# Four graph layers on one core: logit weights by TensorE, three rows of logits spread by TensorE, and layer 0 of two graphs projected ahead of its aggregation

## The chip, the cores and the metric

The kernel runs on one core of a Trainium2 chip. The metric is the device time of one launch in microseconds (us). Five engines work side by side, each through its own queue in order: TensorE (PE, with its weight loads shown as PEld), VectorE (DVE), ScalarE (ACT), GpSimd (POOL) and SyncE (SP), which here issues every DMA.

## The reference

There are 64 graphs of 256 nodes with 512 features each, all in float32. Each of four layers normalises x, takes the positive part h, computes a graph layer from h and the adjacency matrix, and adds the result to x:

```python
h = jnp.maximum(_layernorm(x, axis=-1), 0.0)
x = x + layer(h, adj, ...)
# layer 0: attention
Wh = h @ W
e = leaky_relu(Wh @ a[:512] + swapaxes(Wh @ a[512:], 1, 2), 0.2)
attention = softmax(where(adj > 0.5, e, -9e15), axis=1)
out0 = elu(attention @ Wh)
# layer 1: normalised adjacency
dh = rsqrt(sum(adj + I, -1));  out1 = relu((dh * (adj + I) * dh) @ h @ kernel1 + bias)
# layer 2: plain
out2 = relu((adj @ h) @ kernel2)        # rows of x that are all zero are masked
# layer 3: mean and self
out3 = relu(concat([h, adj @ h / deg]) @ W3.T)
```

## The kernel before, in words

**Tiles.** A graph is 2 chunks of 128 nodes. x of a graph stays in SBUF (`xs`) through all four layers. A layer 0, 1 or 2 is an aggregation (`aggregate`, L450) and a projection (`project`, L511). The aggregation multiplies h as the stationary operand with the moving 256 columns of the attention or the adjacency, so its result `pt` has features on the partitions, in two PSUM banks; ACT and DVE evict it into `xw` (`left_sums`, L436). The projection multiplies `xw` with the weights in seven products of half size instead of eight (a scheme of Strassen's kind). It needs sums of blocks on both sides: S1 to S4 of `xw` (DVE at L445 and L428, POOL at L432), and the differences T1 to T4N of each weight, which POOL makes once at the start (`weight_sums`, L285, the instructions at L290). Three PSUM banks z, v and y collect the products (L529); ACT keeps copies (L568) and DVE adds (L570). Layer 3 projects first and then aggregates.

**Layer 0.** `norm(0)` gives h0. Four DVE operations (L628) multiply h0 with the rows of `wa`, which is W a spread over all partitions, and sum along the features: the two logits `lg` of each node. One of them must lie as a row on all partitions. `along` (L347) does that: a DVE transpose (L355), a DMA to DRAM (L358), and a DMA that reads the row back to all partitions (L361). Then ACT adds the other logit and takes the leaky relu (L634), DVE masks (L642) and takes the maximum (L645), ACT exponentiates (L649), DVE inverts the sum (L652), ACT scales (L655), and `e` is the attention. `aggregate("h0", "e", 0)` and the projection follow, and `elu0` adds the ELU of the result to x in three pieces, of 256, 256 and 512 columns.

**The logit weights.** `logit_weights` (L253) makes `wa` ahead of everything: it loads W0 a second time in four blocks of rows (L259) and both halves of a, each read to all partitions (L263); eight DVE operations (L270) multiply and sum along a row into columns; eight TensorE transposes of a broadcast column (`spread`, L242, recorded at L244) lay them as rows on all partitions in PSUM, and ACT copies them to `wa` (L282).

**The order of the work.** Nothing is issued where it is written. Each step is registered with `op` (L217): its engine, a planned duration, a function, the keys that it reads and writes. `Plan.place` (L70) then simulates the engines: a planned duration is multiplied by STRETCH of its engine, due times are passed backwards from those of each graph (APART us from graph to graph, the last LAST graphs closer together by LATE), and at each point the engine takes the step that can start first, then the one that is due first; for TensorE a step counts as ready only SPARE us after its inputs. Buffers are given out in the same simulation, from the numbers at L819. Steps are then emitted in order of their planned start, so each engine's order is fixed; the chip's own waits do the rest.

```python
rank = (max(free[eng], ready + spare), not op.urgent, op.due, op.at)
```

Of the kernel before, what the change touches and what calls it, by code (L numbers as in the profile page):

```python
# [11 lines left out]
ALU = mybir.AluOpType  # L12
AX = mybir.AxisListType

P = 128
# [6 lines left out]
HOP = 0.25  # L22
APART = 12.0
LAST, LATE = 2, 0.3

STRETCH = {"DVE": 1.25, "ACT": 1.15, "POOL": 1.2, "PE": 1.0, "DMA": 1.0}
SPARE = 0.15

# [121 lines left out]
def kernel(  # L150
# [21 lines left out]
    nc = tc.nc  # L172
    B, N, F = x.shape
    O = w0.shape[1]
    NC = N // P
# [14 lines left out]
    class Tiles:  # L190
# [5 lines left out]
        def declare(self, name, shape, pool=None, tag=None):  # L196
            tag = pool or tag or name
            self.tiles[name] = Buffered(shape, tag, f"{name}_{self.name}")
# [43 lines left out]
    def spread(to, col):  # L242

        nc.tensor.transpose(to, col.to_broadcast([P, P]), ident)  # L244
# [7 lines left out]

    def logit_weights():  # L253
        me = Tiles("l", 0.0)
        op, declare = me.op, me.declare
        declare("wa_col", [P, 2, FC])
        for k in range(FC):
            declare(f"w0{k}", [P, O], tag="xw")
            op("DMA", 256, lambda g, k=k: nc.sync.dma_start(  # L259
                g[f"w0{k}"], w0[k * P : (k + 1) * P, :]), (), [f"w0{k}"])  # L260
        for j in range(2):
            declare(f"a{j}", [P, O], tag="ex512")
            op("DMA", 256, lambda g, j=j: nc.sync.dma_start(  # L263
                g[f"a{j}"],
                a0[j * O : (j + 1) * O, :].rearrange("o u -> u o").to_broadcast([P, O])),
               (), [f"a{j}"])
        for k in range(FC):
            for j in range(2):
                declare(f"junk{j}{k}", [P, O], tag="mva")
                op("DVE", 0.77, lambda g, j=j, k=k: nc.vector.scalar_tensor_tensor(  # L270
                    g[f"junk{j}{k}"], g[f"w0{k}"], 1.0, g[f"a{j}"], ALU.mult, ALU.mult,
                    accum_out=g["wa_col"][:, j, k : k + 1]),
                   [f"w0{k}", f"a{j}"], [f"junk{j}{k}", f"wa_col.{j}"])
        for j in range(2):
            declare(f"pw{j}", [P, F], "ps")

            def go(g, j=j):
                for k in range(FC):
                    spread(g[f"pw{j}"][:, k * P : (k + 1) * P], g["wa_col"][:, j, k : k + 1])

            op("PE", 0.6, go, [f"wa_col.{j}", "=ident"], [f"pw{j}"])
            op("ACT", 0.59, lambda g, j=j: nc.scalar.copy(wa[:, j, :], g[f"pw{j}"]),  # L282
               [f"pw{j}"], [f"=wa{j}"])

    def weight_sums(op, n, b12):  # L285
# [8 lines left out]
    def weight(n, w):  # L294
# [3 lines left out]
        for at, i, j in ((B11, 0, 0), (None, 0, 1), (B22, 1, 1), (B21, 1, 0)):  # L298
# [5 lines left out]
                  (), ["b12" if at is None else f"=wb{n}.{at}"])  # L304
        weight_sums(me.op, n, "b12")

    def last_weight():
# [34 lines left out]
    def graph(b):  # L342
# [283 lines left out]
        for j in range(2):  # L626
            for c in range(NC):
# [3 lines left out]
                   [f"h0.{c}", f"=wa{j}"], ["e.0", "e.1", f"lg.{j}{c}"])  # L631
        along("pl", lambda g: g["lg"][:, 0, :], ["lg.00", "lg.01"])
        for c in range(NC):
# [20 lines left out]
        for c in range(NC):  # L654
            op("ACT", 0.5, lambda g, c=c: nc.scalar.activation(  # L655
                g["e"][:, c, :], g["e"][:, c, :], AF.Copy, scale=g["den"][:, c : c + 1]),
               [f"e.{c}", f"den.{c}"], [f"e.{c}", "e"])
        aggregate("h0", "e", 0)

# [15 lines left out]
        first, second, third = pieces(0)  # L675
        project([Weighted("xw0", 0)], 0, plain_keep, 0.38, plain_total, lambda _: elu0(*first, "a"))
        elu0(*second, "b")
        elu0(*third, "c")
        norm(1, "dh")
# [131 lines left out]
    constants()  # L811
    logit_weights()
    weight(0, w0)
# [3 lines left out]
    for b in range(B):  # L817
        graph(b)
    buffers = dict(  # L819
        xs=7, a_nat=1, ab=1, aT=6, h=3, mva=6, xw=5, c=3, off=1, junk=1, ex256=3, ex512=2,  # L820
        wa_col=1, turned=1, row=4, pl=1, pr=1, hb=1, ps=8,
    )
# [36 lines left out]
```

## Time and profile before

| | |
|---|---|
| median of 3 runs | 2843.36 us (2842.63 to 2843.51) |
| the profiled execution: time, span from first to last instruction | 2844.11 us, 2842.3 us |
| granted TensorE clock | 0.999 |
| DMA over the span | 161.07 MB, 57 GB/s; 189 GB/s from 0 to 5 us, 311 GB/s from 5 to 10 us |
| TensorE busy from 0 to 30 us | 3.75 us |
| TensorE busy from 142 to 2700 us | all but 0.4 us |

The page of a profile gives each engine's busy time and its share of the span. A row of a group or of the timeline names the engine, the line, the operation and its operands, how many there are and how long; in square brackets stands the idle time before it and what ended it. A float32 product of TensorE is recorded as two instructions; a transpose is one. A busy time of TensorE includes the drain of each instruction, so the distance from start to start (0.22 us for 256 columns) is the time that counts, not the 379 ns of a record.

### The profile page before, as it was taken

To read this page: it belongs to the slowest core of one execution; us is meant where nothing else is said; L and a number is where in the kernel's file an instruction comes from. 1 tells how busy PE (TensorE), PEld (TensorE's weight loads), DVE (VectorE), ACT (ScalarE), POOL (GpSimd) and SP (SyncE) were. 2 spreads that over 40 slices of the span, in tenths; PEclk is the share of its full clock that TensorE was granted. 3 is DMA by queue.
4 is the path that set the end of the run, shared out by engine and by line. 5 is a ranking of instruction groups with operands and counts; after the bars stand their busy time and mean duration, and the time that the engine had idled before them with its cause. 6 is when DMAs were issued, how large, how long until landed. Compare 5 with 4: busy or idle time off the path is not lost.

```text
span 2842.3 us, 43136 instructions
## 1 busy us (share of the span) xinstructions
PE 2802.9 (99%) x12968; PEld 2461.2 (87%) x12968; DVE 1963.5 (69%) x5136; ACT 1691.1 (59%) x4115; POOL 1246.4 (44%) x2331
## 2 busy tenths in 40 slices
PE   5999999999999999999999999999999999999999
PEld 4888888888888888888888888888888888888887
DVE  7767676676766767667676667676776766667654
ACT  5766566556666566566565665665665656556552
POOL 6554344444444444444444444444444444443432
PEclk9999999999999999999999999999999999999999
DMA  7122331222222222222222222222222222222112
GB/s 199 20 51 61 72 70 40 62 53 53 58 53 58 56 49 59 61 45 61 46 62 56 47 66 55 48 59 56 53 59 47 60 53 40 58 49 44 39 34 52
DMA packets 495062, 161.07 MB, mean 57 GB/s; under 512 B 424816, under 2 KB 460656, under 8 KB 494832
## 3 DMA queue, kind: packets, MB, share of 16 engines
q1 hardware_dynamic: 494832, 158.33, 24.0%
q8 instruction: 105, 1.72, 0.3%
q14 instruction: 125, 1.02, 0.1%
HBM read 90.96 MB, written 33.69 MB: 44 GB/s over the span
## 4 chain that ended last, share of the span: by engine, by line
PE 97%; DMA 1%; DVE 1%; POOL 0%; SPq 0%; issue 0%; ACT 0%; DVEq 0%; POOLq 0%
PE pz L529 43%; PE pt L460 23%; PE pv L529 21%; PE py L529 11%; POOL wb L290 0%; DMA xs<-in_x_dram 0%; DMA ab<-in_adj_dram 0%; DVE e L628 0%; SPq L603 0%; DMA wb<-in_L_gnn_W_dram 0%; DVE e L642 0%; DMA pr<-dpr 0%; DVE xw L445 0%; SPq L259 0%; DVE stats L385 0%
## 5 line engine op out<-in xcount | busy, mean ns | idle before, releaser
L529 PE MATMUL pz<-wb,xw 128*128 128x256 f32 x3072 | 767.9, 379 | 2.5 <-DVE c L694 0.6
L529 PEld LDWEIGHTS pz<-wb,xw 128*128 128x128 f32 x3072 | 582.9, 190 | 83.9 <-ACT c L568 1.1
L568 ACT COPY c<-pz 128x256 f32<-128x256 f32 x576 | 213.6, 371 | 550.9 <-PE pz L529 550.3
L529 PE MATMUL pz<-wb,hw 128*128 128x256 f32 x2048 | 524.8, 379 | 0.9 <-ACT c L568 0.9
L432 POOL TENSOR_TENSOR xw<-xw 128x256 f32<-128x256 f32 x384 | 296.1, 791 | 482.1 <-DVE xw L428 326.5
L529 PEld LDWEIGHTS pz<-wb,hw 128*128 128x128 f32 x2048 | 389.0, 190 | 54.5 <-ACT c L568 1.7
L422 ACT ACTIVATE h<-xs,nb,rstd 128x512 f32<-128x512 f32 x512 | 402.1, 809 | 45.5 <-POOL nb L419 39.7
L529 PE MATMUL pv<-wb,xw 128*128 128x256 f32 x1536 | 393.7, 379 | 1.7 <-DVE xw L445 1.1
L529 PEld LDWEIGHTS pv<-wb,xw 128*128 128x128 f32 x1536 | 291.5, 190 | 41.9 <-POOL wb L290 1.5
L570 DVE TENSOR_TENSOR c<-pv,c 128x256 f32<-128x256 f32 x384 | 161.7, 421 | 222.3 <-PE pv L529 150.4
L401 ACT ACTIVATE h<-xs,mv 128x512 f32<-128x512 f32 x384 | 275.4, 718 | 56.1 <-POOL mv L395 36.3
L529 PE MATMUL pv<-wb,hw 128*128 128x256 f32 x1024 | 262.8, 379 | 0.0
L460 PE MATMUL pt<-e,h 128*128 128x256 f32 x1024 | 233.8, 381 | 15.8 <-ACT e L655 15.8
L460 PE MATMUL pt<-aT,h 128*128 128x256 f32 x1024 | 236.9, 379 | 0.0
L460 PE MATMUL pt<-ahT,h 128*128 128x256 f32 x1024 | 233.1, 379 | 0.0
L460 PEld LDWEIGHTS pt<-e,h 128*128 128x128 f32 x1024 | 195.8, 191 | 43.0 <-ACT e L655 16.1
L409 POOL TENSOR_TENSOR rstd<-rstd,minus_half 128x2 f32<-128x2 f32 x256 | 215.9, 843 | 17.3
L460 PEld LDWEIGHTS pt<-aT,h 128*128 128x128 f32 x1024 | 194.5, 190 | 26.7 <-ACT h L422 0.3
L460 PEld LDWEIGHTS pt<-ahT,h 128*128 128x128 f32 x1024 | 194.6, 190 | 26.5
L529 PEld LDWEIGHTS pv<-wb,hw 128*128 128x128 f32 x1024 | 194.5, 190 | 26.5
L628 DVE SCALAR_TENSOR_TENSOR e<-h,wa 128x512 f32<-128x512 f32 x256 | 196.7, 768 | 16.5 <-ACT h L422 5.8
L529 PE MATMUL py<-wb,xw 128*128 128x256 f32 x768 | 197.1, 379 | 0.0
(116 smaller groups left out, 4460.8 us busy)
## 6 DMA issues: line engine op xcount, KB each, us to landing
xs<-in_x_dram SPq DMA_DIRECT2D x64, 512.0 KB
hw<-hb SPq DMA_DIRECT2D x1024, 32.0 KB
out_dram<-xs SPq DMA_DIRECT2D x64, 512.0 KB
ab<-in_adj_dram SPq DMA_DIRECT2D x512, 32.0 KB
a_nat<-in_adj_dram SPq DMA_DIRECT2D x64, 256.0 KB
pl<-dpl SPq DMA_DIRECT2D x64, 128.0 KB
pr<-dpr SPq DMA_DIRECT2D x64, 128.0 KB
w3n_w<-in_L_gnn_W_dram SPq DMA_DIRECT2D x4, 512.0 KB
```

The source lines that it names most:

```text
L401: op("ACT", 1.0, lambda g, c=c: nc.scalar.activation(g[h][:, c, :], g["xs"][:, c, :], AF.Square, bias=g[mv][:, 0, c : c + 1], accum_out=g[ ...
L409: op("POOL", 0.72, lambda g: nc.gpsimd.tensor_tensor(g[rs], g[rs], minus_half, ALU.pow), [rs, "=half"], [rs])
L422: op("ACT", 0.81, lambda g, c=c: nc.scalar.activation(g[h][:, c, :], g["xs"][:, c, :], AF.Relu, bias=g[nb][:, c : c + 1], scale=g[rs][:, c ...
L432: op("POOL", 0.85, lambda g, i=i, o=o: nc.gpsimd.tensor_tensor(g[xw][:, o], g[xw][:, i], g[xw][:, S2], ALU.subtract), put(i, S2), put(o), ...
L460: nc.tensor.matmul(g[pt][:, kk, :], lhsT=g[h][:, c, k * P : (k + 1) * P], rhs=g[moving][:, c, :], start=(c == 0), stop=(c == NC - 1),)
L529: nc.tensor.matmul(g[t], lhsT=o.left(g, left, k), rhs=o.right(g, right, k), start=start and n == 0, stop=n == len(parts) - 1, skip_group_c ...
L568: return "ACT", lambda g, to, block: nc.scalar.copy(to, block)
L570: plain_total = (0.43, lambda g, i, to, block: nc.vector.tensor_tensor(to, block, to, ALU.add))
L628: op("DVE", 0.77, lambda g, j=j, c=c: nc.vector.scalar_tensor_tensor(g["e"].rearrange("p c n -> p (c n)"), g["h0"][:, c, :], 1.0, wa[:, j, ...
```

## The change

W a: `logit_weights` is now called from `weight` for W0, after its differences. It loads a once, as 8 rows of 128, turns them to columns by one transpose, transposes the 16 blocks of W0 (from the tiles that the projection uses), ACT evicts these in four copies, and eight products of 512 columns, with a column of a broadcast as the stationary operand, give W a on all partitions; ACT copies the two halves to `wa`. The second load of W0, the broadcast loads of a and the DVE operations are gone.

Rows of logits: for the first three graphs (ON_PE), two TensorE transposes of a broadcast column put the row into PSUM, where `along` was. Other graphs keep `along`.

Layer 0 of the first two graphs (FIRST): h0 is transposed by TensorE (16 transposes) in the place of the aggregation, then evicted and projected by the same `left_sums` and `project`, into `wh` in SBUF; then for each half of the nodes two products with the attention as the stationary operand and 512 columns of `wh` as the moving one give the layer's result in PSUM, and the ELU takes it in two pieces of 512 columns.

Planner: APART 12 to 14, LAST 2 to 4, smaller STRETCH for DVE, ACT and POOL, SPARE 0.15 to 0.3; one buffer of the tag `ex256` less.

```diff
@@ -20,11 +20,13 @@
 ALPHA = 0.2
 NEG_INF = -9000000000000000.0
 HOP = 0.25
-APART = 12.0
-LAST, LATE = 2, 0.3
-STRETCH = {"DVE": 1.25, "ACT": 1.15, "POOL": 1.2, "PE": 1.0, "DMA": 1.0}
-SPARE = 0.15
+APART = 14.0
+ON_PE = 3
+FIRST = 2
+LAST, LATE = 4, 0.3
+STRETCH = {"DVE": 1.15, "ACT": 1.1, "POOL": 1.15, "PE": 1.0, "DMA": 1.0}
+SPARE = 0.3
@@ -250,38 +252,6 @@
         op("DMA", 256, lambda g: nc.sync.dma_start(
             bias, b1.rearrange("(u o) -> u o", u=1).to_broadcast([P, O])), (), ["=bias"])
-    def logit_weights():
-        me = Tiles("l", 0.0)
-        op, declare = me.op, me.declare
-        declare("wa_col", [P, 2, FC])
-        for k in range(FC):
-            declare(f"w0{k}", [P, O], tag="xw")
-            op("DMA", 256, lambda g, k=k: nc.sync.dma_start(
-                g[f"w0{k}"], w0[k * P : (k + 1) * P, :]), (), [f"w0{k}"])
-        for j in range(2):
-            declare(f"a{j}", [P, O], tag="ex512")
-            op("DMA", 256, lambda g, j=j: nc.sync.dma_start(
-                g[f"a{j}"],
-                a0[j * O : (j + 1) * O, :].rearrange("o u -> u o").to_broadcast([P, O])),
-               (), [f"a{j}"])
-        for k in range(FC):
-            for j in range(2):
-                declare(f"junk{j}{k}", [P, O], tag="mva")
-                op("DVE", 0.77, lambda g, j=j, k=k: nc.vector.scalar_tensor_tensor(
-                    g[f"junk{j}{k}"], g[f"w0{k}"], 1.0, g[f"a{j}"], ALU.mult, ALU.mult,
-                    accum_out=g["wa_col"][:, j, k : k + 1]),
-                   [f"w0{k}", f"a{j}"], [f"junk{j}{k}", f"wa_col.{j}"])
-        for j in range(2):
-            declare(f"pw{j}", [P, F], "ps")
-            def go(g, j=j):
-                for k in range(FC):
-                    spread(g[f"pw{j}"][:, k * P : (k + 1) * P], g["wa_col"][:, j, k : k + 1])
-            op("PE", 0.6, go, [f"wa_col.{j}", "=ident"], [f"pw{j}"])
-            op("ACT", 0.59, lambda g, j=j: nc.scalar.copy(wa[:, j, :], g[f"pw{j}"]),
-               [f"pw{j}"], [f"=wa{j}"])
     def weight_sums(op, n, b12):
         w = wb[n]
         key = lambda i: b12 if i is None else f"=wb{n}.{i}"
@@ -303,6 +273,50 @@
                 g["b12"] if at is None else wb[n][:, at], block),
                   (), ["b12" if at is None else f"=wb{n}.{at}"])
         weight_sums(me.op, n, "b12")
+        if n == 0:
+            logit_weights(me)
+    def logit_weights(me):
+        op, declare = me.op, me.declare
+        OC = O // P
+        declare("a_rows", [2 * OC, P])
+        declare("a_cols", [P, 2 * OC])
+        op("DMA", 4, lambda g: nc.sync.dma_start(
+            g["a_rows"], a0.rearrange("(r p) u -> r (p u)", p=P)), (), ["a_rows"])
+        declare("pa", [P, 2 * OC], "ps")
+        op("PE", 0.15, lambda g: nc.tensor.transpose(
+            g["pa"], g["a_rows"], ident[: 2 * OC, : 2 * OC]), ["a_rows", "=ident"], ["pa"])
+        op("ACT", 0.25, lambda g: nc.scalar.copy(g["a_cols"], g["pa"]), ["pa"], ["a_cols"])
+        blocks = {(0, 0): B11, (0, 1): None, (1, 0): B21, (1, 1): B22}
+        for i in range(OC):
+            declare(f"pw{i}", [P, F], "ps")
+            declare(f"wt{i}", [P, F], tag="aT")
+            for k in range(FC):
+                at = blocks[k // FH, i // (OC // 2)]
+                key = "b12" if at is None else f"=wb0.{at}"
+                def go(g, i=i, k=k, at=at):
+                    block = g["b12"] if at is None else wb[0][:, at]
+                    o = i % (OC // 2) * P
+                    nc.tensor.transpose(
+                        g[f"pw{i}"][:, k * P : (k + 1) * P], block[:, k % FH, o : o + P], ident)
+                op("PE", 0.2, go, [key, "=ident"], [f"pw{i}.{k}"])
+            op("ACT", 0.59, lambda g, i=i: nc.scalar.copy(g[f"wt{i}"], g[f"pw{i}"]),
+               [f"pw{i}.{k}" for k in range(FC)], [f"wt{i}"])
+        for j in range(2):
+            declare(f"pwa{j}", [P, F], "ps")
+            for i in range(OC):
+                op("PE", 0.9, lambda g, i=i, j=j: nc.tensor.matmul(
+                    g[f"pwa{j}"],
+                    lhsT=g["a_cols"][:, j * OC + i : j * OC + i + 1].to_broadcast([P, P]),
+                    rhs=g[f"wt{i}"],
+                    start=i == 0,
+                    stop=i == OC - 1,
+                ), ["a_cols", f"wt{i}"] + ([f"pwa{j}"] if i else []), [f"pwa{j}"])
+            op("ACT", 0.59, lambda g, j=j: nc.scalar.copy(wa[:, j, :], g[f"pwa{j}"]),
+               [f"pwa{j}"], [f"=wa{j}"])
     def last_weight():
@@ -629,7 +643,13 @@
                     g["e"].rearrange("p c n -> p (c n)"), g["h0"][:, c, :], 1.0, wa[:, j, :], ALU.mult, ALU.mult,
                     accum_out=g["lg"][:, j, c : c + 1]),
                    [f"h0.{c}", f"=wa{j}"], ["e.0", "e.1", f"lg.{j}{c}"])
-        along("pl", lambda g: g["lg"][:, 0, :], ["lg.00", "lg.01"])
+        if b < ON_PE:
+            declare("pl", [P, N], "ps")
+            op("PE", 0.23, lambda g: [
+                spread(g["pl"][:, c * P : (c + 1) * P], g["lg"][:, 0, c : c + 1]) for c in range(NC)
+            ], ["lg.00", "lg.01", "=ident"], ["pl"])
+        else:
+            along("pl", lambda g: g["lg"][:, 0, :], ["lg.00", "lg.01"])
         for c in range(NC):
             op("ACT", 0.47, lambda g, c=c: nc.scalar.activation(
                 g["e"][:, c, :], g["pl"], AF.Prelu, bias=g["lg"][:, 1, c : c + 1], alpha=ALPHA),
@@ -655,7 +675,6 @@
             op("ACT", 0.5, lambda g, c=c: nc.scalar.activation(
                 g["e"][:, c, :], g["e"][:, c, :], AF.Copy, scale=g["den"][:, c : c + 1]),
                [f"e.{c}", f"den.{c}"], [f"e.{c}", "e"])
-        aggregate("h0", "e", 0)
         def elu0(i, key, y, y_keys, to, to_keys, n, at, tag):
@@ -673,9 +692,51 @@
                 to(g), g[ex], -1.0, to(g), ALU.add, ALU.add, **kw), [ex], to_keys)
         first, second, third = pieces(0)
-        project([Weighted("xw0", 0)], 0, plain_keep, 0.38, plain_total, lambda _: elu0(*first, "a"))
-        elu0(*second, "b")
-        elu0(*third, "c")
+        if b < FIRST:
+            for half in range(2):
+                pt = f"pt0_{half}"
+                declare(pt, [P, FH, N], "ps")
+                def go(g, half=half, pt=pt):
+                    for k in range(FH):
+                        for c in range(NC):
+                            f0 = (half * FH + k) * P
+                            nc.tensor.transpose(
+                                g[pt][:, k, c * P : (c + 1) * P], g["h0"][:, c, f0 : f0 + P], ident)
+                op("PE", 0.5, go, ["h0.0", "h0.1", "=ident"], [pt])
+            together("pt0_0", "pt0_1")
+            left_sums("pt0_0", "pt0_1", "xw0")
+            declare("wh", [P, NC, O], tag="h")
+            places = {(i, j): (lambda g, i=i, j=j: quarter(g["wh"], i, j), f"wh.{i}{j}")
+                      for i, j in PLACE}
+            project([Weighted("xw0", 0)], 0, plain_keep, 0.38, plain_total,
+                    lambda pz: op("ACT", 0.38, lambda g: nc.scalar.copy(quarter(g["wh"], 1, 0), g[pz]),
+                                  [pz], ["wh.10"], urgent=True), places=places)
+            for i, piece in ((1, second), (0, third)):
+                po = f"po{i}"
+                declare(po, [P, O], "ps")
+                def go(g, i=i, po=po):
+                    for c in range(NC):
+                        nc.tensor.matmul(
+                            g[po],
+                            lhsT=g["e"][:, c, i * P : (i + 1) * P],
+                            rhs=g["wh"][:, c, :],
+                            start=c == 0,
+                            stop=c == NC - 1,
+                        )
+                op("PE", 1.73, go, ["e", "wh.00", "wh.01", "wh.10", "wh.11"], [po])
+                elu0(i, piece[1], lambda g, po=po: g[po], [po],
+                     lambda g, i=i: g["xs"][:, i, :], XS[2 * i : 2 * i + 2], O, piece[-1], "ac"[i])
+            op("POOL", 0.15, lambda g: nc.gpsimd.memset(g["total1"][:, 1:2], 0.0), (), ["total1.10"])
+        else:
+            aggregate("h0", "e", 0)
+            project([Weighted("xw0", 0)], 0, plain_keep, 0.38, plain_total, lambda _: elu0(*first, "a"))
+            elu0(*second, "b")
+            elu0(*third, "c")
         norm(1, "dh")
@@ -809,7 +870,6 @@
     constants()
-    logit_weights()
     weight(0, w0)
     weight(1, w1)
     weight(2, w2)
@@ -817,8 +877,8 @@
     for b in range(B):
         graph(b)
     buffers = dict(
-        xs=7, a_nat=1, ab=1, aT=6, h=3, mva=6, xw=5, c=3, off=1, junk=1, ex256=3, ex512=2,
-        wa_col=1, turned=1, row=4, pl=1, pr=1, hb=1, ps=8,
+        xs=7, a_nat=1, ab=1, aT=6, h=3, mva=6, xw=5, c=3, off=1, junk=1, ex256=2, ex512=2,
+        a_rows=1, a_cols=1, turned=1, row=4, pl=1, pr=1, hb=1, ps=8,
     )
     for tag in ("stats", "total", "mv", "rstd", "nb", "deg", "dh", "rdeg", "lg", "top", "den", "mask"):
         buffers[tag] = 6
```

## The prediction

> **What bounds the kernel now.** I read, in this order, the page (busy shares), the busy time by stretch, TensorE's timeline at the start, its waits, and the timeline of all engines between 14 and 34 us.
>
> ```profile
> PE 2802.9 (99%) x12968; PEld 2461.2 (87%) x12968; DVE 1963.5 (69%) x5136; ACT 1691.1 (59%) x4115; POOL 1246.4 (44%) x2331
> ```
> ```profile
> 10.00:20.00 10.00, 3.31 (x7) 1.27 (x7) 9.23 (x32) 2.69 (x4) 4.35 (x4) 1.00 0.82 234
> 20.00:30.00 10.00, 0.00 (x0) 0.00 (x0) 7.65 (x17) 4.43 (x12) 8.40 (x11) 1.00 0.89 237
> 30.00:40.00 10.00, 6.80 (x22) 5.57 (x23) 7.56 (x17) 5.15 (x13) 9.59 (x12) 1.00 0.78 212
> 40.00:50.00 10.00, 7.33 (x31) 5.24 (x31) 9.83 (x19) 5.77 (x20) 8.18 (x12) 1.00 0.83 233
> ...
> 1000.00:2000.00 1000.00, 1000.00 (x4635) 880.32 (x4634) 699.75 (x1833) 601.92 (x1466) 435.84 (x826) 1.00 0.24 55
> ```
> Columns: stretch, length, then busy us of PE, PEld, DVE, ACT, POOL, clock, DMA share, GB/s. From 142 to 2690 us TensorE never waits; only the start and the last few us leave it idle. So the change can gain only at the start, and it can lose anywhere.
>
> ```profile
> 16.89 0.47 PE L244 MATMUL pw_l<-ident,wa_col_l 128*128 128x128 f32 x1 [1.81 <-DVE junk_l L270]
> 33.20 5.62 PE L460 MATMUL pt<-e,h 128*128 128x256 f32 x16 [15.84 <-ACT e L655]
> 38.66 1.03 PE L529 MATMUL pz<-wb,xw 128*128 128x256 f32 x4
> ...
> 48.44 3.62 PE L460 MATMUL pt<-e,h 128*128 128x256 f32 x16
> 51.89 1.03 PE L529 MATMUL pz<-wb,xw 128*128 128x256 f32 x4
> ```
> ```profile
> PE pt L460 <- ACT e L655: 15.8, 1, 15.8
> PE pw_l L244 <- DVE junk_l L270: 13.2, 5, 9.5
> ```
> The first useful product starts at 33.20, when the attention of graph 0 is done; before it TensorE runs only eight transposes for W a.
>
> ```profile
> 16.01 0.25 DVE L355 STREAM_TRANSPOSE tpl<-lg 128x64 f32<-128x64 f32 x1
> ...
> 16.53 0.67 SPq L358 DMA_DIRECT2D dpl<-tpl  x1
> ...
> 21.88 0.34 SPq L361 DMA_DIRECT2D pl<-dpl  x1
> ...
> 26.22 0.91 ACT L634 ACTIVATE e<-pl,lg 128x256 f32<-128x256 f32 x2 [0.34 <-DMA pl<-dpl]
> ...
> 27.37 0.65 DVE L642 SCALAR_TENSOR_TENSOR e<-off,e 128x512 f32<-128x512 f32 x1
> ...
> 32.66 0.89 ACT L655 ACTIVATE e<-e,den 128x256 f32<-128x256 f32 x2
> ```
> Here the reader sees why: the logits cross to all partitions through DRAM, 16.01 to 26.22, and then max, exponent and division take another 7 us.
>
> **A ledger of TensorE.** 3245 instructions in 700 us (2000 to 2700) give 0.2157 us per pass of 256 columns (a product has two passes). 12,928 such passes make 2789.2, and 32 transposes of the last weight at 0.109 (eight in 0.87) make 3.5: 2792.7 of work. The last product ends at about 2837.4, which leaves 4.9. So 2842.3 = 33.2 before the first product + 2792.7 + 4.9 + 11.5 of gaps. Of the 11.5, 2.0 is a slow first burst (16 passes take 38.66 - 33.20 = 5.46; those at 48.44 take 3.45); the rest lies nearly all before 91.
>
> **What the Trainium skill says.** (1) "TensorE: Matmul & The Clock Gate", Part 1: an idle TensorE runs at half clock until about 3.4 us of activity. The slow burst agrees. (2) Its Part 4 says that transposes don't count as activity. The lone pw_l transposes have a mean of 470 ns, the later pw_w ones 273; that fits, but doesn't separate clock from spacing. (3) "DMA: Bandwidth & Descriptors", Anatomy of one DMA: some 2 us fixed, mostly the write receipt. The trip through DRAM has two such in series and took 10.2 us with its queueing. (4) "GPSIMD Engine Reference", section 8: POOL shares SBUF interfaces with VectorE. L642 took 0.65 us at 27.37, but 1.65 at 39.63 beside a weight difference of POOL.
>
> **The change, part by part.**
>
> *W a on TensorE.* It removes eight L270 operations from VectorE: 8 x (0.678 + 0.083) = 6.1 us, in 8.69 to 16.8, where VectorE is the busy engine. It removes six loads of 256 KB, 1.5 MB, from queues that carry some 235 GB/s then: 6 us of transfer. It adds a load of 4 KB, 16 transposes (1.7 at 0.109; up to 7.5 at the lone 0.47), and 8 products of 512 columns, 16 passes of 2 x 0.2157: 6.9 us warm. ACT gets four more evictions of 0.59 and one small one, 2.6, where it is half idle. Replacing the eight old transposes saves nothing on the path. Is W a ready earlier? x of graph 0 and W0 are 1.5 MB; 189 GB/s to 5 us and 311 after it land that at about 6.8, if they are issued first. Transposes and evictions to 9.5, four products partly cold to 14, copy to 14.6; the second half at 18. The old copies end at 13.1 and 18.0. So not earlier: what it frees is VectorE and the loads.
>
> *Rows by TensorE, graphs 0 to 2.* Removes per graph a 0.24 turn, two DMAs, and the trip of 10.2. Adds two transposes, 0.22, so 0.65 in all, and takes a PSUM bank until the two Prelu have read it. The spread waits on VectorE's two sums; everything planned behind it on TensorE waits too, between 0 and 1.5 us (two L628) per graph. I take 0.5. The second sum of graph 0 (19.5, after wa1) then ends last, not the row: Prelu at 19.5 instead of 26.2; with the 7.0 from there to the product, e comes at about 25.5 to 26.5.
>
> *Layer 0 of graphs 0 and 1 by nodes.* The 16 aggregation passes of 256 (3.45) become 8 of 512 (3.45). The 14 products stay, 6.04. New are 16 transposes each, 1.74, so 3.5. What moves is the projection: it needs h, the weights and POOL's four differences (about 1.5 each after W0 lands: 13 us), not e. So 12.1 us of work can run before e. VectorE's ELU pieces drop from three to two: per graph four passes of 0.69 against two sets of 0.42 + 0.42 + 0.69, 0.4 us with the reads. Each graph holds one more of three h buffers; graph 2's h then waits for graph 0's sums, which end at 19.7, before it is late. ex256 loses a buffer: in steady state ACT waits there for VectorE already, off the path; I cost it at nothing, and up to 0.2 us a graph if that cover is gone.
>
> *Planner constants.* All 64 graphs are reordered, every queue with them, SP's and POOL's too. The stretch on VectorE falls from 1.25 to 1.15, and 0.3 us of slack ahead of a TensorE step stands where 0.15 stood. The steady hw sums (L769 686 ns, L428 639) are planned at 0.43: over the new plan by 0.19 and 0.14, together about the new 0.3. VectorE has 30% free, so I take no cost; bounds from -1 (the end) to +0.3 us per graph, 19 us.
>
> **The sum.** New TensorE work is 1.7 + 6.9 + 0.65 + 3.5 = 12.8. New ledger: start 6.8 + cold 3 (bounds 2 to 6) + 12.8 + 2792.7 + 4.9 = 2820.2 plus gaps. Equal time would need 22.1 of gaps. Before e, 18.7 us stand against 19.5 of work (W a 8.6 + 3 cold, graph 0's transposes and projection 7.8), some of it waiting for POOL and evictions: 4 of gap. After e, I take the 9.5 of before: the same chains feed the same layers. Total 2833.7, so 8.6 less. A cross-check from VectorE, over 90% busy in the tens and forties: it is relieved of 6.1 + 0.7 + 0.8 = 7.6. Late next are POOL (8.4 to 9.6 of 10 us busy between 20 and 40 with weight differences) and VectorE. The profiled execution took 2844.11 for a span of 2842.3; the median of the runs is 0.75 lower. So 2833.7 + 1.8 - 0.75 = 2834.75; I state 2834.5, own range 2829 to 2838.5.
>
> **Rivals.** *Nearly gapless*: projections of both graphs fill the wait, gaps are 6: 2826.2 span, 2827 median. For it: 24 us of work free of e. Against: VectorE has no slack between 40 and 60. Lower bound 2824.
> *The feeders don't move*: POOL's sixteen differences (24 us at 1.5) and the loads decide when layer 1 can run; 33.6 to 36 is such a chain. Then only some 3 us are left: 2840.5, range 2838 to 2845. For it: POOL's lines above. Against: W0 lands earlier, so the chain starts earlier.
> *Slower by thin margins*: the plan, made with faster helpers, makes TensorE wait a little in each graph. At 0.3 us it is 19 - 8.6 = +10.6: 2854. It cancels the gain from 0.14 us per graph and is measurably slower from 0.22. For it: the hw sums over plan. Against: not one steady wait before, and more slack ahead of TensorE.
> *The change doesn't do what it says*: the planner may still set projections behind e, by due times. It then gives the third case's time and is counted there.
>
> **Chances.** Forecast 0.51, nearly gapless 0.17, feeders 0.19, thin margins 0.13. About 0.2%, 5.7 us, is what a measurement can tell from no change: faster means under 2837.7. Forecast gives 0.47 faster and 0.04 same; gapless 0.17 faster; feeders 0.01 faster, 0.17 same, 0.01 slower; margins 0.13 slower. Faster 0.65, same 0.21, slower 0.14. The range leaves out half of the margins' case and the outer ends: 2825 to 2846.
>
> **What would show it.** Right: no DMA from dpl to pl for graphs 0 to 2, first products of L529's kind before 15 us, the first attention product near 26, VectorE without L270, no wait of TensorE between 142 and 2690. Wrong: W a's products waiting long for evictions, a long gap of TensorE after 26, or small waits repeated in each graph.

## The result and the profile after

The changed kernel takes 2833.26 us (median of 7 runs, 2832.73 to 2834.06); the kernel before took 2843.41 beside it (7 runs, 2842.63 to 2844.41). The ratio is 0.9964, interval 0.9953 to 0.9976: 10.1 us faster, 1.2 us below the forecast of 2834.5. The profiled execution took 2832.82 us for a span of 2831.0, so 1.8 lies around the span, as before.

Busy shares on the page of after:

```profile
PE 2813.3 (99%) x12999; PEld 2464.8 (87%) x12999; DVE 1911.0 (68%) x5111; ACT 1707.6 (60%) x4118; POOL 1202.9 (42%) x2333
```

TensorE does more (31 instructions, 10 us) in less time. Busy time by stretch of after (columns as in the prediction):

```profile
10.00:20.00 10.00, 10.00 (x26) 4.59 (x26) 3.75 (x9) 4.15 (x9) 4.48 (x6) 1.00 0.82 248
20.00:30.00 10.00, 8.12 (x40) 5.94 (x38) 9.25 (x24) 6.41 (x18) 7.66 (x11) 1.00 0.90 300
30.00:40.00 10.00, 9.17 (x40) 6.26 (x38) 9.79 (x22) 6.53 (x19) 9.41 (x11) 1.00 0.73 210
40.00:50.00 10.00, 7.65 (x29) 4.38 (x28) 8.35 (x25) 7.41 (x21) 9.34 (x17) 1.00 0.55 144
...
1000.00:2000.00 1000.00, 1000.00 (x4635) 880.32 (x4634) 682.16 (x1839) 609.59 (x1469) 420.33 (x828) 1.00 0.24 55
```

The middle is the same row for TensorE: 4635 instructions in 1000 us, no wait. The difference is the start: between 20 and 30 us, where TensorE had stood still, it is busy for 8.12. Its timeline in after:

```profile
3.55 1.09 PE L302 MATMUL pw_w<-ident,wb 128*128 128x128 f32 x4 [3.55 <-DMA wb<-in_L_gnn_W_dram]
...
9.72 1.91 PE L311 MATMUL pwa_w<-wt_w,a_cols_w 128*128 128x512 f32 x2
...
11.86 6.57 PE L311 MATMUL pwa_w<-wt_w,a_cols_w 128*128 128x512 f32 x12
18.27 0.60 PE L705 MATMUL pt<-ident,h 128*128 128x128 f32 x4
18.70 1.02 PE L311 MATMUL pwa_w<-wt_w,a_cols_w 128*128 128x512 f32 x2
...
20.00 1.03 PE L543 MATMUL pz<-wb,xw 128*128 128x256 f32 x4
20.86 0.38 PE L246 MATMUL pl<-ident,lg 128*128 128x128 f32 x2
...
30.02 3.70 PE L723 MATMUL po<-wh,e 128*128 128x512 f32 x8
```

W a's products begin at 9.72, the projection of graph 0 at 20.00, the row is spread by TensorE at 20.86 in place of the trip through DRAM, and the attention is used at 30.02 (33.20 before). TensorE's waits in after, over the whole run (us in total, times, longest):

```profile
PE pw_w L302 <- DMA wb<-in_L_gnn_W_dram: 4.9, 2, 3.6
PE pz L543 <- ACT wh L582: 2.1, 3, 0.8
PE pa_w L288 <- DMA a_rows_w<-in_L_gnn_a_dram: 1.1, 1, 1.1
```

After the loads, the longest wait left is 0.9 us; before, one alone was 15.8.

**The ledger, redone from the trace.** For every pair of TensorE instructions in a row, the distance of their starts less the duration of the first at full clock (0.21575 us for 256 columns, 0.4315 for 512, 0.108 for a transpose) is time lost to waits, to half clock and to other gaps. I use this for all runs below.

| profiled run | first instruction | lost to 90 us | lost 90 to 2700 | lost after 2700 | work | last start to end | span |
|---|---|---|---|---|---|---|---|
| before | 9.5 | 30.8 | 1.9 | 1.5 | 2793.3 | 5.3 | 2842.3 |
| after | 3.6 | 16.7 | 1.0 | 0.8 | 2803.6 | 5.4 | 2831.0 |

The start improves by 5.9 + 14.1 = 20.0, the middle and the end by 1.6; the work grows by 10.3 and the last term by 0.1: 11.2 less, and the spans differ by 11.3.

### The profile page after: what moved, and what is told of

Same layout as the page of the kernel before. It is cut to its first block, busy times and chain, and to the rows that moved or that the text cites. A ratio compares the mean times of both kernels' runs of the same rounds, so it can differ in the third digit from the quotient of the medians.

```text
span 2831.0 us, 42966 instructions
## 1 busy us (share of the span) xinstructions
PE 2813.3 (99%) x12999; PEld 2464.8 (87%) x12999; DVE 1911.0 (68%) x5111; ACT 1707.6 (60%) x4118; POOL 1202.9 (42%) x2333
## 4 chain that ended last, share of the span: by engine, by line
PE 98%; POOL 0%; DVE 0%; DMA 0%; ACT 0%; issue 0%; SPq 0%; DVEq 0%; POOLq 0%
PE pz L543 43%; PE pt L474 23%; PE pv L543 21%; PE py L543 11%; PE pwa_w L311 0%; POOL wb L260 0%; DMA a_rows_w<-in_L_gnn_a_dram 0%; PE po L723 0%; ACT h L436 0%; PE pw_w L302 0%; DMA pl<-dpl 0%; PE pt L705 0%; SPq L272 0%; DMA dpl<-tpl 0%; POOL xw L446 0%
## 5 line engine op out<-in xcount | busy, mean ns | idle before, releaser
L436 ACT ACTIVATE h<-xs,nb,rstd 128x512 f32<-128x512 f32 x512 | 398.4, 809 | 10.3 <-POOL nb L433 7.2
L474 PE MATMUL pt<-ahT,h 128*128 128x256 f32 x1024 | 240.9, 379 | 0.9 <-ACT h L436 0.9
L474 PE MATMUL pt<-e,h 128*128 128x256 f32 x992 | 225.0, 379 | 0.4 <-ACT e L675 0.4
L409 POOL TENSOR_SCALAR mv<-total 128x1 f32<-128x1 f32 x192 | 111.7, 582 | 261.2 <-DVE xs L691 134.0
L454 ACT COPY xw<-pt 128x512 f32<-128x512 f32 x192 | 112.4, 585 | 178.7 <-PE pt L474 178.6
L543 PEld LDWEIGHTS pv<-wb,hw 128*128 128x128 f32 x1024 | 194.6, 190 | 26.5
L474 PEld LDWEIGHTS pt<-e,h 128*128 128x128 f32 x992 | 188.3, 190 | 26.4 <-ACT e L675 0.8
L459 DVE TENSOR_TENSOR xw<-pt,xw 128x256 f32<-128x256 f32 x192 | 80.2, 418 | 178.4 <-ACT xw L454 171.2
```

The costliest lines, as they stand in the source:

```text
L409: op("POOL", 0.3, lambda g: nc.gpsimd.tensor_scalar(g[mv][:, 0, 1:2], g[t][:, 1:2], g[t][:, 2:3], -1.0 / F, ALU.add, ALU.mult), [f"{t}.10" ...
L436: op("ACT", 0.81, lambda g, c=c: nc.scalar.activation(g[h][:, c, :], g["xs"][:, c, :], AF.Relu, bias=g[nb][:, c : c + 1], scale=g[rs][:, c ...
L454: op("ACT", 0.59, lambda g: nc.scalar.copy(g[xw][:, A12 : A22 + 1 : A22 - A12].rearrange("p h k n -> p k h n"), g[hi].rearrange("p k (h n) ...
L459: op("DVE", 0.43, lambda g: nc.vector.tensor_tensor(g[xw][:, S1], g[lo][:, :, P:], g[xw][:, A22], ALU.add), [lo] + put(A22), put(S1), urge ...
L474: nc.tensor.matmul(g[pt][:, kk, :], lhsT=g[h][:, c, k * P : (k + 1) * P], rhs=g[moving][:, c, :], start=(c == 0), stop=(c == NC - 1),)
L543: nc.tensor.matmul(g[t], lhsT=o.left(g, left, k), rhs=o.right(g, right, k), start=start and n == 0, stop=n == len(parts) - 1, skip_group_c ...
```

## The experiments

My theory when these began was the forecast's: the gain is TensorE's work that no longer waits for `e`, the planner's constants give next to nothing, and each part has a price of its own. The rivals: the constants or the order that the planner happens to draw make the gain; or VectorE's relief does. Later kernels put these apart. In each batch the kernel before took 2843.2 to 2843.6. No kernel here leaves out a part of the computation; some add work whose result isn't read.

**First batch: undo one part, let the planner place the rest.**

```diff
-ON_PE = 3
+ON_PE = 0
```

> The changed kernel with the rows of logits of the first three graphs sent through DRAM again; all else as changed. My theory (each of the three parts feeds TensorE earlier, the planner's constants do next to nothing): the row of graph 0 comes some 9 us later, its attention product moves from 30 us to about 36; the projections of two graphs cover part of it, so 4 us are lost: 2837 us. Rival (the planner's constants make the gain): no change, 2833 us. Rival (rows are the whole gain): 2842 us.

2851.11 us (2848.94 to 2852.34), ratio to before 1.0028 (1.0017 to 1.0039). TensorE's longest waits in it:

```profile
PE pt L474 <- ACT h L436: 8.3, 2, 7.5
PE pw_w L340 <- DMA w3n_w<-in_L_gnn_W_dram: 6.0, 1, 6.0
```

```diff
-FIRST = 2
+FIRST = 0
```

> The changed kernel with layer 0 of the first two graphs aggregated first again; all else as changed. My theory: TensorE has no work free of the attention between W a and some 28 us, 12.1 us of projections come behind it, 3.5 us of transposes are saved: 6 to 8 us are lost, 2840 us. Rival (the planner's constants): 2833 us. Rival (VectorE sets the pace of the start, so that TensorE's order there is worth nothing): 2833 us or, with the transposes saved, 2830 us.

2850.91 us (2848.28 to 2852.70), ratio 1.0027 (1.0017 to 1.0036). Its timeline of TensorE:

```profile
27.87 5.22 PE L474 MATMUL pt<-e,h 128*128 128x256 f32 x16 [7.40 <-ACT e L675]
...
87.19 6.27 PE L474 MATMUL pt<-ahT,h 128*128 128x256 f32 x16 [6.57 <-ACT h L436]
```

The 16 passes that take 3.45 us at full clock ("warm") take 5.1 from start to next start after the first of these waits: the granted clock is 0.50 from 25 to 30 us, so part of the burst runs at half clock ("cold").

```diff
-APART = 14.0
+APART = 12.0
-LAST, LATE = 4, 0.3
+LAST, LATE = 2, 0.3
-STRETCH = {"DVE": 1.15, "ACT": 1.1, "POOL": 1.15, "PE": 1.0, "DMA": 1.0}
+STRETCH = {"DVE": 1.25, "ACT": 1.15, "POOL": 1.2, "PE": 1.0, "DMA": 1.0}
-SPARE = 0.3
+SPARE = 0.15
```

The third kernel, undo_constants, has this edit and the third `ex256` buffer again; the fourth, constants_alone, has the reverse of the constants in the kernel before.

> The changed kernel planned with the constants of before (APART, LAST, STRETCH, SPARE, and three buffers of the tag ex256). My theory: no wait of TensorE between 142 and 2690 us, the start within 2 us of the changed kernel: 2833 to 2835 us. Rival (the constants make the gain): 2843 us.

> The kernel before planned with the new constants, nothing else changed. My theory: 2842 to 2845 us, no waits after 142 us. Rival (the constants make the gain): 2833 us. Rival of the thin margins, in its mild form: small waits repeat in each graph, 2850 us or more.

undo_constants: 2849.91 us (2846.52 to 2852.43), ratio 1.0022 (1.0014 to 1.0031). constants_alone: 2851.59 (2849.97 to 2853.26), ratio 1.0029 (1.0019 to 1.0040). The long waits in TensorE's timeline of undo_constants:

```profile
30.34 6.63 PE L723 MATMUL po<-wh,e 128*128 128x512 f32 x8 [3.21 <-ACT e L675]
85.25 6.48 PE L474 MATMUL pt<-ahT,h 128*128 128x256 f32 x16 [6.72 <-ACT b_w L347]
```

and of constants_alone:

```profile
29.48 6.32 PE L460 MATMUL pt<-e,h 128*128 128x256 f32 x16 [12.54 <-ACT e L655]
88.60 5.78 PE L460 MATMUL pt<-ahT,h 128*128 128x256 f32 x16 [5.66 <-ACT h L422]
```

| profiled run | first instruction | lost to 90 us | 90 to 2700 | after 2700 |
|---|---|---|---|---|
| undo_rows | 3.6 | 33.2 | 1.0 | 0.8 |
| undo_nodes | 3.7 | 34.3 | 3.0 | 0.8 |
| undo_constants | 3.7 | 31.5 | 3.2 | 1.5 |
| constants_alone | 9.1 | 38.0 | 2.4 | 0.8 |

Each takes one part away, or adds one part alone, and each ends slower than both kernels. They lose it in the first 90 us, the most of it in single waits of 3 to 12 us and the slow bursts behind them; the thin margins of the prediction (0.3 us in each graph, 19 in all) are in none of them, for 90 to 2700 holds 3.2 us at most. So "the constants give next to nothing" fell, and so did a price for each part: without the constants the other parts make +6.7 us on before, the constants alone +8.4, both together -10.1. Each edit also draws a new order of everything, and it brings long waits far from the part taken away: before 45 us in undo_rows, and before 85 to 89 us in all four. To price a part, the order has to be held.

**Second batch: after's own order.** rows_same_order keeps the other instructions of after in their order and sends the row through DRAM in the place of the two transposes:

```diff
-            op("PE", 0.23, lambda g: [
-                spread(g["pl"][:, c * P : (c + 1) * P], g["lg"][:, 0, c : c + 1]) for c in range(NC)
-            ], ["lg.00", "lg.01", "=ident"], ["pl"])
+            op("PE", 0.23, through_dram, ["lg.00", "lg.01", "=ident"], ["pl"])
```

`through_dram` makes the DVE transpose, the DMA to DRAM and the DMA back, as `along` does; the leaky relu reads the tile that comes back.

> The changed kernel in its own planned order, but at the place of the spread of graphs 0 to 2 the row goes by a turn on VectorE and two DMAs through DRAM, as before; nothing else is planned anew. Theory A (a part of the change is worth what it moves on the path, and the 18 us that the re-planned undoing lost come mostly from stalls of the new order): the leaky relu of graph 0 waits some 6 us more, ScalarE's and TensorE's queues behind it too, graphs 1 and 2 less: 2838 to 2842 us. Theory B (rows on TensorE are worth the whole 18 us): 2850 us.

2848.95 us (2846.55 to 2852.15), ratio 1.0020 (1.0012 to 1.0028): 15.7 over after. In its timeline of all engines, ACT waits for graph 0's row, and the next thing on ACT is the eviction `wh` that TensorE needs:

```profile
25.78 0.91 ACT L664 ACTIVATE e<-plf,lg 128x256 f32<-128x256 f32 x2 [4.57 <-DMA plf<-rowf]
26.59 0.35 ACT L582 COPY wh<-pz 128x256 f32<-128x256 f32 x1
```

ACT's waits for all three rows together (us in total, times, longest):

```profile
ACT e L664 <- DMA plf<-rowf: 15.4, 3, 6.3
```

TensorE's timeline of the same kernel shows what the first two cost:

```profile
27.09 2.05 PE L543 MATMUL pz<-wb,xw 128*128 128x256 f32 x4 [3.97 <-ACT wh L582]
...
47.73 2.04 PE L543 MATMUL pz<-wb,xw 128*128 128x256 f32 x4 [6.11 <-ACT wh L582]
```

The four passes behind each of these waits take over 2.0 us instead of 1.03: they also run cold. The third row ends in a wait of 3.3 us before 70.98. Graph 0's leaky relu starts only 2.4 us later than in after (25.78 for 23.35), but the rows of graphs 1 and 2 come late too, and each time the engine that waits holds a queue. In after ACT waits 1.5 and 1.3 us ahead of the same step, and not at all for the third row. Lost to 90 us: 31.7 for 16.7. SyncE's queue is held as well: the load of x that stands behind the first row is issued at 21.91 instead of 16.55. What share of the 15.7 that has was not separated. This is nearer to the 2850 of theory B than to the 2838 to 2842 of theory A.

nodes_pool_later is undo_nodes with four of POOL's weight differences moved up to 6 us back in the order:

```diff
     plan.place(buffers)
+    for o in reversed(moved):
+        limit = min(h.start for h in o.heirs) - 0.01
+        o.start = max(o.start, min(o.start + 6.0, limit))
```

> The kernel with layer 0 of the first two graphs aggregated first, in the planned order of that run, but POOL's first differences of the last weight stand some 6 us of planned time later in POOL's queue. Theory A (the wait of 6.6 us near 87 us is made by those differences ahead of a layer normalisation in POOL's queue): the wait shrinks to 3 us or less, the cold burst after it too: 2845 us or less. Theory B (it is ScalarE's queue or the data that makes it): no change, 2851 us.

2850.82 us (2846.51 to 2852.65), ratio 1.0024 (1.0013 to 1.0035), no change. It tells nothing: the differences that I moved run near 98 us; those beside the wait at 87, at 75.5 to 80, are of the other half of the last weight. The wait of 6.6 us is still there. In its trace DVE's additions to x end there at 80 to 82, POOL's steps of the norm follow, and ACT makes `h` from 84.6; what would shorten that was not found.

loads_back issues the six old loads of 256 KB again, behind those of W0 and a, into tiles that nobody reads:

```diff
+            for k in range(FC):
+                old = sb.tile([P, O], F32, tag=f"xw{k + 1}", bufs=1, name=f"old_w{k}")
+                nc.sync.dma_start(old, w0[k * P : (k + 1) * P, :])
+            for j in range(2):
+                old = sb.tile([P, O], F32, tag=f"ex512{j}", bufs=1, name=f"old_a{j}")
+                nc.sync.dma_start(old, a0[j * O : (j + 1) * O, :].rearrange(
+                    "o u -> u o").to_broadcast([P, O]))
```

vector_back puts eight VectorE operations of the old kind back, one pair behind each copy of `wt`:

```diff
+                for j in range(2):
...
+                    nc.vector.scalar_tensor_tensor(
+                        junk, flat(B11), 1.0, flat(B21), ALU.mult, ALU.mult,
+                        accum_out=wa_old[:, j, i : i + 1])
```

> The changed kernel in its own order with the six loads of 256 KB of the old W a put back behind the loads of W0, into buffers that nothing reads. If the 1.5 MB less on the queues are a part of the gain: the adjacency and x of graphs 0 to 2 come 5 to 6 us later, 3 to 6 us lost: 2836 to 2839 us. If the loads have slack in the new order: 2833 us, within 1.

> The changed kernel in its own order with eight products with sums of 128 x 512 put back on VectorE between the evictions of W0's transposes, as the old W a had them; their results are not used. If VectorE's relief of 6.1 us is a part of the gain, as my cross-check of the prediction had it: 3 to 6 us lost, 2836 to 2839 us. If it is not (VectorE waits 5.1 us for wa in the changed kernel, and is only 3.75 of 10 us busy between 10 and 20): at most 1.5 us lost, 2833 to 2835 us.

loads_back: 2837.05 us (2835.62 to 2838.61), ratio 0.9977 (0.9968 to 0.9986), 3.8 over after. vector_back: 2835.00 (2834.22 to 2836.42), ratio 0.9971 (0.9959 to 0.9982), 1.7 over after. The one long wait that TensorE's timeline of loads_back has and after has not:

```profile
41.99 2.05 PE L552 MATMUL pz<-wb,xw 128*128 128x256 f32 x4 [3.96 <-ACT wh L591]
```

and the two of vector_back:

```profile
38.94 1.31 PE L553 MATMUL pz<-wb,xw 128*128 128x256 f32 x4 [2.20 <-POOL mv L419]
...
41.83 1.94 PE L350 MATMUL pw_w<-ident,w3n_w 128*128 128x128 f32 x8 [1.58 <-DMA w3n_w<-in_L_gnn_W_dram]
```

Ahead of the wait in loads_back, ACT waits 3.0 us for a load of the adjacency, until 41.08, so here the loads do reach the path. By the medians the 1.5 MB of loads cost more than the 6 us of VectorE work, though the two intervals overlap; VectorE has room there now (3.75 of 10 us busy between 10 and 20 in after).

**Third batch: the end, the order, the clock.** undo_last takes back only how the last graphs are due (`LAST` 4 to 2); hop_024 takes nothing back and only draws another order:

```diff
-LAST, LATE = 4, 0.3
+LAST, LATE = 2, 0.3
```

```diff
-HOP = 0.25
+HOP = 0.24
```

> The changed kernel with LAST back at 2; only the order of the last graphs differs. My theory (the end is worth at most 1 us; the gain sits in the start): 2833 to 2834.5 us, and the start as in the changed kernel. Rival (the end carries a part of the 10 us): 2836 us or more.

> The changed kernel with the planner's HOP at 0.24 in the place of 0.25, a change without meaning for the chip that makes the planner draw another order from the start on. Theory A (the three parts make the gain in whatever order): 2831 to 2837 us. Theory B (the gain of 10 us belongs to one order whose start has no gap of over 1 us; other orders of the same parts hit gaps of 3 to 8 us, and a slow clock after each): 2840 to 2852 us.

undo_last: 2836.87 us (2835.24 to 2837.38), ratio 0.9975 (0.9965 to 0.9985), 3.6 over after. hop_024: 2844.35 (2841.75 to 2845.97), ratio 1.0003 (0.9995 to 1.0011): the whole gain is gone. TensorE's timeline at the end of undo_last:

```profile
2781.11 1.10 PE L543 MATMUL pz<-wb,hw 128*128 128x256 f32 x4 [1.62 <-DMA hw<-hb]
2787.42 1.13 PE L543 MATMUL pz<-wb,hw 128*128 128x256 f32 x4 [0.46 <-ACT y L582]
```

and of hop_024:

```profile
2800.46 1.10 PE L543 MATMUL pz<-wb,hw 128*128 128x256 f32 x4 [2.10 <-DMA hw<-hb]
...
2815.13 1.13 PE L543 MATMUL pz<-wb,hw 128*128 128x256 f32 x4 [0.46 <-ACT c L582]
```

Both stand in the last layer (its input is `hw`): a product waits for an eviction, 0.46 us each time, and once for a DMA. I take it that few graphs are left there whose work could be put between; no run shows that by itself. Lost to 90 us: 16.2 and 16.8 (after 16.7). Lost after 2700: 5.6 and 9.1 (after 0.8). So hop_024 bears out that the size of the gain hangs on the drawn order, but I had looked for it in the start, and it is in the end. The small loss at the start stays in both of these orders. That hop_024's median lies 2.6 over its profiled run stays unexplained.

nodes_filled is undo_nodes with products of the identity (28 and 26) ahead of its two long waits, so that TensorE isn't idle in them:

```diff
+                    if (b, l) in FILL:
+                        for _ in range(FILL.pop((b, l))):
+                            nc.tensor.matmul(
+                                g[pt][:, 0, :P], lhsT=ident, rhs=ident, start=True, stop=True)
```

> The kernel with layer 0 of the first two graphs aggregated first, in the order of its run, with 28 and 26 products of the identity ahead of the two long waits of TensorE (7.4 us near 28, 6.6 us near 87): they fill the gaps and change nothing of the results. Theory (a gap costs its idle time and then a slow clock as well): the idle time stays, the slow bursts (5.2 in place of 3.45 us, and what follows) go: 4 to 6 us less than the 2850.9 of that kernel, 2845 to 2847 us. If the slow clock costs next to nothing: 2850 us, or more if the filling delays products.

2848.64 us (2846.57 to 2851.25, 21 runs), ratio 1.0018 (1.0011 to 1.0024): 2.3 under undo_nodes, 3.2 in the profiled pair; I had looked for 4 to 6. Its timeline of TensorE, beside the fence of undo_nodes above:

```profile
21.37 6.42 PE L474 MATMUL pt<-ident 128*128 128x128 f32 x56
28.93 3.72 PE L479 MATMUL pt<-e,h 128*128 128x256 f32 x16 [1.15 <-ACT e L680]
```

The burst is warm again (28.93 to the next start at 32.49 is 3.56). In undo_nodes the distance from 27.87 was 5.06 (the next start is 32.93). So a long wait cost itself and some 1.5 us of half clock behind it, 2.5 after the one at 87.19 (6.27 for 3.72); the rest of undo_nodes' loss is in the main idle time. Not all of the 3.2 is the filling's: the burst at 47.57 in undo_nodes takes 5.31, and the same burst at 48.59 in nodes_filled 3.62, though nothing was put ahead of it and the waits before the two are alike (2.72 and 2.32). A wait's length alone does not tell whether the burst behind it is cold.

warm_a_first is after with three edits: the 4 KB load of a first, ten products of the identity ahead of W0's first transposes, and four ahead of a's:

```diff
             make_identity(nc, ident)
+            warm(10)
...
+            warm(4)
             nc.tensor.transpose(g["pa"], g["a_rows"], ident[: 2 * OC, : 2 * OC])
...
+    ahead[0].start = -1.0
```

> The changed kernel in its own order with two additions: the 4 KB of a are loaded ahead of everything, and TensorE runs ten products of the identity before the first transposes and four before a is turned, so that its clock is up when the products of W a start. In the changed kernel these start at 9.72 us, and 14 passes of them take 8.55 us where 14 x 0.43 = 6.0 would do. Expected: W a ready 2 to 3 us earlier, the attention of graph 0 likewise, 1 to 2.5 us off the time: 2831 to 2832 us. If the start is bound by the loads or VectorE after that: 2833 us.

2830.65 us (2829.64 to 2833.81, 5 runs), ratio 0.9956 (0.9943 to 0.9968); profiled span 2828.8 for 2831.0. Four of five runs lie below all of after's, though the intervals of the two ratios overlap. Its timeline of TensorE:

```profile
9.04 1.02 PE L325 MATMUL pwa_w<-wt_w,a_cols_w 128*128 128x512 f32 x2
...
10.12 5.32 PE L325 MATMUL pwa_w<-wt_w,a_cols_w 128*128 128x512 f32 x12
...
27.03 3.70 PE L737 MATMUL po<-wh,e 128*128 128x512 f32 x8
```

The first two passes take 0.86 us from start to start instead of 1.71, the twelve 5.15 instead of 6.41, and the attention is used at 27.03 instead of 30.02. A new wait of 2.0 us for `wh` before 36.41 takes part of it back. The 5.15 can't be put down to the warming. In hop_024, which has no such products, the clock is up from 11.58 us:

```profile
9.97 1.77 PE L311 MATMUL pwa_w<-wt_w,a_cols_w 128*128 128x512 f32 x2
11.58 0.38 PE L302 MATMUL pw_w<-ident,wb 128*128 128x128 f32 x2
11.80 5.32 PE L311 MATMUL pwa_w<-wt_w,a_cols_w 128*128 128x512 f32 x12
16.95 0.60 PE L705 MATMUL pt<-ident,h 128*128 128x128 f32 x4
```

Its twelve passes take 5.15 too, and so do those of undo_last. In the profiled runs of the eleven kernels that make W a by TensorE without warming they take 5.15 to 6.41, and after's is the longest. Only warm_a_first has its first two passes warm. Its three edits were not tried one by one.

## Why the prediction was right, and where its steps were not

**Where the gain can lie: right.** TensorE's loss from 90 to 2700 us is 1.0 us for 1.9; all the gain is at the start, as said. "Thin margins" didn't come, nor did "feeders don't move".

**The sum: near, with terms that err both ways.** The span is 2831.0 where 2833.7 was predicted; the medians are nearer (1.2), since the profiled run of before lay 0.75 over its median and that of after lies 0.44 under it. Predicted for the start, the cold clock and the gaps were 6.8 + 3 + 13.5 = 23.3; measured are 3.55 + 18.5 = 22.0 (18.5 is 16.7 + 1.0 + 0.8): the start 3.2 better, the rest 2 worse. That so near a number came out is in part luck: these errors cancel, and hop_024, with the same parts and another order, takes 2844.35, outside the range of 2829 to 2838.5. Work: predicted 12.8 of new TensorE work, measured 11.1 (10.3 more than before, which had 0.8 of transposes that are gone). The failed term is "New are 16 transposes each, 1.74, so 3.5": it is 8 for each graph (2 chunks by 4 blocks), 16 in all, and at 0.108 us these are 1.7. The other terms (W a 6.9 warm, 16 transposes of W0, six of rows) are as costed.

**"Start 6.8": 3.55.** I let the first transpose wait for all 1.5 MB. It needs one block of W0. TensorE then waits 1.3 us for the next block and 1.1 for a, until 8.19.

**"Four products partly cold to 14, copy to 14.6; the second half at 18": too early.** The copies are at 17.61 and 19.76. The weight loads of after show why; their spacing tells the clock:

```profile
12.71 0.34 PEld L311 LDWEIGHTS pwa_w<-wt_w,a_cols_w 128*128 128x128 f32 x1 [0.52 <-issue]
13.56 0.34 PEld L311 LDWEIGHTS pwa_w<-wt_w,a_cols_w 128*128 128x128 f32 x1 [0.52 <-issue]
14.40 0.19 PEld L311 LDWEIGHTS pwa_w<-wt_w,a_cols_w 128*128 128x128 f32 x1 [0.50 <-ACT h L436]
14.83 0.19 PEld L311 LDWEIGHTS pwa_w<-wt_w,a_cols_w 128*128 128x128 f32 x1 [0.24 <-issue]
```

Up to about 14.3 a pass of 512 columns takes 0.85 us, then 0.43. The first five passes are cold, 2.1 us; I knew of the cold clock, but let the transposes from 3.55 on warm it. The Trainium skill, "TensorE: Matmul & The Clock Gate", Part 4, which the prediction cites, says that they don't count. Here the first product is cold after six us that hold only transposes and two waits; but the last stretch of transposes without a wait is 1.5 us long, so no run separates "doesn't count" from "too short". warm_a_first, where products took that place, is warm from its first pass of W a. Part 1 of that page gives about 3.4 us of activity until the full clock; in after it came about 4.6 us after the first product, but the other ten kernels with this start have it after some 1.4 to 3.9 (hop_024 1.5), with two to four cold passes. The clock's share of this start thus differs from run to run, and after's profiled run has the most of it.

**"The second sum of graph 0 then ends last, not the row", e at 25.5 to 26.5: the kind right, the time 3.5 to 4.5 late.** All engines of after:

```profile
17.61 0.58 ACT L318 COPY wa<-pwa_w 128x512 f32<-128x512 f32 x1 [3.51 <-PE pwa_w L311]
18.23 0.69 DVE L642 SCALAR_TENSOR_TENSOR e<-h,wa 128x512 f32<-128x512 f32 x1 [5.09 <-ACT wa L318]
...
23.35 0.84 ACT L654 ACTIVATE e<-pl,lg 128x256 f32<-128x256 f32 x2 [1.50 <-DVE e L642]
```

The leaky relu waits for VectorE's sums, and these wait 5.09 us for `wa`. So VectorE's relief is not even used there, and the cross-check "relieved of 7.6" found the right size by chance: vector_back measures 1.7 for the eight operations.

**"First products before 15 us": wrong, 20.00.** I let the projection run before W a. The plan puts W a first, and graph 0's transposes between its last passes. The projection still fills what was idle: 7.1 us of work lie between 20.00 and 30.02, with 2.9 lost.

**"4 of gap" before e, 9.5 after it.** Up to 30.02 are lost 6.8 + 2.9 = 9.7 (predicted 3 + 4), after it 8.7. That the same chains feed the same layers afterwards holds for some orders and not for others: from the attention to 90 us after loses 6.9, the same parts in undo_last 7.0 and in hop_024 8.5, but with the old constants (undo_constants) 20.7.

**"Planner constants: no cost, -1 to +0.3 per graph": right against before, wrong as a part.** From 90 us on no more was lost than before (1.0 for 1.9), and the end went from 1.5 to 0.8, within the bound. But with `LAST` at 2 this kernel would lose 5.6 there, and with the old constants 15 us more at the start. I costed the constants as a small offset of each graph; they choose the order, and the order at the two ends can cost as much as the whole gain of 10.1 (14.8 us more lost at the start in undo_constants, 8.3 more at the end in hop_024).

Open are the price of each part under an order made for it (projecting two graphs first was tried only under a new order), and the cause of the wait at 87 us in undo_nodes, where the test missed its aim.

## What to carry to other kernels

Where a planner writes the order, taking out one part draws everything anew: price a part in the order of the whole kernel, and draw some neighbouring orders (a constant by 4%) before a gain of half a per cent is put down to the edit. When a transfer is taken off a path, look at which engine waits for it and what that engine has queued behind: here three rows for which ACT waited 15.4 us cost 15.7. At the start, a TensorE that has nothing to do yet may be worth warming up on products (2.6 us here by the medians, with overlapping intervals). And one trace of a cold start is not enough to cost it: the same start had two to five cold passes.

## What the hardware showed that I had not expected

In after the granted clock reads 1.00 for the first 20 us, while the spacing of TensorE's passes (0.85 us per pass of 512 columns, then 0.43) shows half clock up to 14.3; in these traces the column tells of half clock only from a later drop on (0.50 after the 7.4 us wait in undo_nodes). Float32 products of the identity, some 0.11 us each pass, kept the clock up through 6 us in nodes_filled. The 4 KB load of a, issued behind the blocks of W0, lands only at 8.19, and TensorE waits for it. VectorE's product of h0 with `wa` (L642 of after) took 0.69 us at 18.23 and 1.65 at 29.93, where POOL runs differences: the sharing that the prediction cites from "GPSIMD Engine Reference" of the Trainium skill, section 8, is seen again.
